# Reflections of a QR in three pieces a step instead of five or four, and a wider spacing of those pieces

## The chip, the core and the metric

The kernel runs on one core of a Trainium2 chip. The metric is device time in microseconds (us), the median of three runs; lower is better. Everything is float32. The core's engines, as the profile names them: PE (TensorE, matrix products), DVE (VectorE), ACT (ScalarE), POOL (GpSimd), and SP, whose queue issues most transfers. Each takes its instructions in the order in which the program leaves them; they wait for one another through semaphores.

## The reference, cut to what matters

Four blocks work one after the other on x (4 batches x 512 tokens x 288 features), with one condition vector for each batch: a transformer block with a mixture of four experts (two chosen for each token), a transformer block with a dense MLP, a rotation within a subspace, and another transformer block. The change touches only the third:

```python
def _L2_cond_ref(x, cond, P, W, b):
    U, _ = jnp.linalg.qr(P)                  # P is 288 x 64
    R = _rotation(cond, W, b)                # expm of a skew 64 x 64 matrix
    z = jnp.einsum('btn,nd->btd', x, U)
    z_rot = jnp.einsum('btd,bde->bte', z, R)
    return x + jnp.einsum('btd,nd->btn', z_rot - z, U)
```

U and R do not depend on x. So the kernel computes them beside the first two blocks. U comes from Householder reflections, 64 of them. For each, one needs the norm of what is left of a column (a sum of squares, then a square root, taken as a power of 0.5), a few scalars, and then the reflection of all later columns.

## The kernel before, in words

**Main work.** The attention of each block runs in 16 groups (4 batches x 4 groups of heads). A group has 8 slots (`k`), and each slot has four score products: two whose row maxima VectorE takes (line 875), two whose exponentials ScalarE takes (line 887). The scores rotate through four PSUM banks (tag `sc`); everything else on TensorE rotates through three (`de`). The products stand in an order fixed by hand: `mm` chains each matmul to the one before it. The first block's experts (`Experts`) work off 19 items of 256 gathered rows each. For an item the first layer is 9 products of 256 columns, each over two full blocks of features and a rest, and the second is 2 x 9 products of 288 columns. Their weights, `e0w`, and rows, `e0xs`, are fetched by indirect transfers that GpSimd issues (line 1818). The results are stored by SP (line 1904).

**Beside-work.** Two lists of generators, `beside` and `aside`, hold work that is done in between. `tick` (line 772) advances the first generator of `beside` to its next `yield`, and with `both` that of `aside` too. An attention ticks four times in each group, in slots 1, 3, 5 and 7, and four times in its first and last; that is 68 ticks. `Feed.went` counts the columns that the MLP or the experts stream, those counted being the products over full blocks of features, and ticks each time that `pace` columns have gone by. In the experts `pace` is 985 and `both` is true; in the dense MLPs it is 1000 and false. Item 0 of the experts is worked off without ticks. A piece of work emitted in a tick goes into each engine's queue at that place among the main work. `beside_of` and `in_turn` tie the first vector instruction of a piece, or the power on GpSimd, to what was last put on that engine by the main work; the other instructions are placed by a scheduler, which keeps dependencies and roughly the order of the program.

`beside` holds `rotation()`: the reflections (`reflections`, 64 columns), then U itself from the kept vectors (`subspace`, 64 steps), then a small product for each batch. The second half of the first block's modulation is put in front of it in group 4 of the first attention and takes five ticks; the last block's modulation stands behind it. `aside` holds the matrix exponential (`exponential`) and the second block's modulation. Beside-work that is left when the second block ends is drained there.

**One reflection**, `k`, in `reflections`: lines 604 to 607 form the sum of squares `rest` (by `dots`, line 555), `n2` and the sign; line 609 takes the power on GpSimd (`nrm`); lines 614 to 619 compute scalars on VectorE and leave two of them beside the row in `pT`; `reflector` (line 545) has SP spread that row over the partitions into `v`; two ticks later `reflect` reads `v` (line 549 first, then 555, 572 and 573). `inside[0]` is true while an attention runs. So a reflection takes five ticks inside an attention and four outside.

Of the kernel before, what the change touches and what calls it, by code (L numbers as in the profile page):

```python
# [45 lines left out]
def kernel(ctx: ExitStack, tc: tile.TileContext, a: dict, out: bass.AP):  # L46
# [21 lines left out]
    def bank(tag, name):  # L68
        return psum.tile([P, 512], F32, tag=tag, name=name, bufs=banks[tag])
# [30 lines left out]
    def beside_of(engine, instruction):  # L100
        if engine in taken:
            ordered(instruction.ins, taken[engine])

    def in_turn(engine, instruction):

        beside_of(engine, instruction)
        take(engine, instruction)
# [433 lines left out]
    def reflector(n, k):  # L541

        v = bgp.tile([RK, C + 2], F32, tag="v", name=f"{n}_{k}", bufs=4)
        r = RK - 1 - k
        nc.sync.dma_start(v[0:r, 0 : C + 2 - k], spread(pT[r : r + 1, k : C + 2], r))
        return v
# [5 lines left out]
    def dots(k, m, v, n):  # L552
        junk = bgp.tile([RK, C], F32, tag="junk", name=f"junk_{k}", bufs=1)
        w = small.tile([RK, 1], F32, tag="w", name=f"w_{k}")
        ins = nc.vector.tensor_tensor_reduce(
            out=junk[0:n, 0 : m.shape[1]],
            in0=m,
            in1=v,
            scale=1.0,
            scalar=0.0,  # L560
            op0=ALU.mult,
            op1=ALU.add,
            accum_out=w[0:n],
        )
        return w[0:n], ins

    def reflect(k, m, v, n):

        c = headed(k, v, n)
        w, _ = dots(k, m[0:n, k:C], v[0:n, 0 : C - k], n)  # L570
        w2 = small.tile([RK, 1], F32, tag="w2", name=f"w2_{k}")
        nc.vector.scalar_tensor_tensor(w2[0:n], w, -1.0, c, ALU.mult, ALU.mult)
        nc.vector.scalar_tensor_tensor(
            m[0:n, k:C], v[0:n, 0 : C - k], w2[0:n], m[0:n, k:C], ALU.mult, ALU.add
        )
# [3 lines left out]
    def reflections():  # L579

        nc.gpsimd.memset(back, 0.0)
        nc.gpsimd.affine_select(
            out=back,
            in_=back,
            compare_op=ALU.not_equal,
            fill=1.0,
            base=1 - RK,
            pattern=[[1, RK]],
            channel_multiplier=1,
        )  # L590
        ps = bank("de", "psback")
        nc.tensor.matmul(ps[0:RK, 0:C], lhsT=back, rhs=pT[:, 0:C], start=True, stop=True)
        nc.vector.tensor_copy(pT[:, 0:C], ps[0:RK, 0:C])
        for k in range(RK):
            n = RK - k

            def one(name):
                return small.tile([RK, 1], F32, tag=name, name=f"{name}_{k}")[0:n]


            alpha, tail = pT[0:n, k : k + 1], pT[0:n, k + 1 : C]
            hd, c = pT[0:n, C : C + 1], pT[0:n, C + 1 : C + 2]
            n2, nrm, sgn = one("n2"), one("nrm"), one("sgn")
            rest, ins = dots(k, tail, tail, n)
            beside_of("DVE", ins)
            nc.vector.scalar_tensor_tensor(n2, alpha, alpha, rest, ALU.mult, ALU.add)  # L606
            nc.vector.tensor_scalar(sgn, alpha, 0.0, 2.0, ALU.is_ge, ALU.mult)
            yield
            in_turn("POOL", nc.gpsimd.tensor_tensor(nrm, n2, phalf[0:n], ALU.pow))  # L609
            yield  # L610


            sn, den, rden = one("sn"), one("den"), one("rden")
            beside_of("DVE", nc.vector.scalar_tensor_tensor(sn, sgn, -1.0, nrm, ALU.add, ALU.mult))
            nc.vector.tensor_add(hd, alpha, sn)
            nc.vector.tensor_mul(den, sn, hd)
            nc.vector.tensor_scalar_max(den, den, TINY)
            nc.vector.reciprocal(rden, den)
            nc.vector.scalar_tensor_tensor(c, rest, 0.0, rden, ALU.is_gt, ALU.mult)
            if n > 1:  # L620
                v = reflector("v", k)
                yield
                yield
                reflect(k, pT, v, n - 1)
                if inside[0]:
                    yield

    def subspace():

# [118 lines left out]
    def rotation():  # L748
        yield from reflections()
        yield from subspace()  # L750
        for b in range(B):
            ps = bank("de", f"psue_{b}")
            for kc in range(KC):
                nc.tensor.matmul(
                    ps[0:CP, kc * RK : (kc + 1) * RK],
                    lhsT=uT[halves[b // HB], kc * CP : (kc + 1) * CP],
                    rhs=ef[halves[b // HB], b % HB, :],
                    start=True,
                    stop=True,
                )  # L760
            nc.vector.tensor_copy(
                ue[:, b, :, :],
                ps[0:CP, 0 : KC * RK].rearrange("p (k j) -> p k j", j=RK),
            )
            yield
# [4 lines left out]
    inside = [False]  # L770
# [436 lines left out]
    class Feed:  # L1207
# [7 lines left out]
        pace, both = 1200, False  # L1215
# [141 lines left out]
    class Dense(Feed):  # L1357


        pace = 1000  # L1360
# [47 lines left out]
    class Experts(Feed):  # L1408
# [5 lines left out]

        pace, both = 985, True
        width = SW
        loads_from, loads_every, loads_at = 2, 1, (0, 2, 4, 6)
        last_pieces = ("XXX", "XX", "", "AAA", "")  # L1420
# [846 lines left out]
```

## Time and profile before

| what | us |
|---|---|
| median of three runs | 2022.97 (2016.03 to 2024.35) |
| the profiled execution | 2016.98 |
| its span, first to last instruction | 2015.0 |
| TensorE busy / mean granted clock | 1913.5 / 0.975 |
| VectorE busy | 1076.7 |
| ScalarE busy | 746.6 |
| GpSimd busy | 539.9 |
| first attention | about 30 to 419 |
| experts | 419 to 925 |
| second attention | 925 to 1310 |
| its dense MLP | to 1460 |
| rotation of x | to 1495 |
| third attention | 1495 to 1850 |
| its dense MLP | to 2015 |

The stages overlap a little at their ends. In the profile a line starts with the engine or with the tile that is written and read: `v<-pT` is the transfer that spreads a row. "A <- B: t, n, m" in a list of waits means that A waited for B for t us in all, n times, at most m us. A line of busy time by stretch gives for each engine the busy us and, in brackets, the instructions, in the order PE, PEld (loading of weights), DVE, ACT, POOL; then the clock granted to TensorE as a share of the full one, the share of DMA engines that were busy, and GB/s. A float32 matmul stands in the profile as two records. A line of a timeline starts with the start and the duration; in square brackets stand the idle time of the engine just ahead of it and what ended it.

### The profile page before, as it was taken

How to read it: one execution, taken by the hardware profiler on the slowest of the kernel's cores; microseconds unless marked ns; L12 is line 12 of the kernel's file. 1: busy time of each engine (PE TensorE's matmuls, PEld its weight loads, DVE VectorE, ACT ScalarE, POOL GpSimd, SP SyncE). 2: the span in 40 equal slices, each digit the busy share in tenths (PEclk: the TensorE clock that was granted, in tenths of full speed). 3: DMA queues.
4: the chain of work that ended last, by engine and by line, in shares of the span. 5: the costliest groups of instructions: out<-in, count | busy, mean ns of one | idle time of the engine just before them, and what ended most of it. 6: DMA issues, size and time to landing. Idle time of an engine off the chain costs nothing. (4 is left out here: it accounts for less than half of the span.)

```text
span 2015.0 us, 28809 instructions
## 1 busy us (share of the span) xinstructions
PE 1913.5 (95%) x10602; PEld 1008.9 (50%) x10602; DVE 1076.7 (53%) x3129; ACT 746.6 (37%) x1367; POOL 539.9 (27%) x776
## 2 busy tenths in 40 slices
PE   7999999998889899899999999999999999999998
PEld 4434443365556667675334443456554344433555
DVE  5666777623434333446777777454155666554211
ACT  1554555332211222232555544511124555555220
POOL 4111121443233445652332122211400211213101
PEclk9999999898889999899999999999999999999999
DMA  7521121346444665651111111220000111111000
GB/s 155 118 54 21 22 45 46 106 117 195 138 138 148 197 203 179 187 183 37 42 44 38 36 37 40 56 61 21 21 1 10 28 29 36 28 26 23 19 15 24
DMA packets 95166, 147.27 MB, mean 73 GB/s; under 512 B 33267, under 2 KB 72798, under 8 KB 95026
## 3 DMA queue, kind: packets, MB, share of 16 engines
q1 hardware_dynamic: 68690, 66.16, 14.3%
q0 software_dynamic: 26224, 79.27, 13.2%
q8 instruction: 84, 1.38, 0.3%
q14 instruction: 56, 0.46, 0.1%
q10 hardware_dynamic: 112, 0.01, 0.0%
HBM read 114.66 MB, written 20.54 MB: 67 GB/s over the span
## 5 line engine op out<-in xcount | busy, mean ns | idle before, releaser
L875 DVE TENSOR_REDUCE max<-a3m 128x1 f32<-128x512 f32 x256 | 164.6, 685 | 128.1 <-PE a3s L78 120.8
L78 PE MATMUL e0h<-e0hT,e0w 128*128 128x256 f32 (+1 forms) x1026 | 213.6, 416 | 13.1 <-DMA e0w<-w1c,wrow 10.2
L875 DVE TENSOR_REDUCE max<-a0m 128x1 f32<-128x512 f32 x256 | 165.3, 683 | 90.2 <-PE a0s L78 78.1
L875 DVE TENSOR_REDUCE max<-a1m 128x1 f32<-128x512 f32 x256 | 165.7, 684 | 75.3 <-PE a1s L78 68.0
L887 ACT ACTIVATE a0p<-a0s 128x512 f32<-128x512 f32 x256 | 140.2, 596 | 144.5 <-PE a0s L78 144.1
L887 ACT ACTIVATE a1p<-a1s 128x512 f32<-128x512 f32 x256 | 140.9, 596 | 139.4 <-PE a1s L78 139.2
L887 ACT ACTIVATE a3p<-a3s 128x512 f32<-128x512 f32 x256 | 140.0, 596 | 137.6 <-PE a3s L78 137.6
L78 PEld LDWEIGHTS e0h<-e0hT,e0w 128*128 128x128 f32 (+1 forms) x1026 | 149.6, 196 | 70.0 <-issue 47.2
L78 PE MATMUL e0o<-e0w,e0hm 128*128 128x288 f32 x648 | 178.6, 427 | 0.1
L78 PE MATMUL a0m<-a0qk,a0qk 32*128 32x512 f32 x512 | 159.1, 645 | 7.9 <-DVE max L875 6.8
L78 PE MATMUL a1m<-a1qk,a1qk 32*128 32x512 f32 x512 | 157.5, 640 | 7.8 <-DVE max L875 6.5
L78 PE MATMUL a0s<-a0qk,a0qk 32*128 32x512 f32 x512 | 161.0, 653 | 0.0
L78 PE MATMUL a1s<-a1qk,a1qk 32*128 32x512 f32 x512 | 158.4, 640 | 0.2 <-DVE u L549 0.2
L78 PE MATMUL a3m<-a3qk,a3qk 32*128 32x512 f32 x512 | 151.2, 643 | 6.8 <-DVE max L875 5.5
L78 PE MATMUL a3s<-a3qk,a3qk 32*128 32x512 f32 x512 | 153.0, 644 | 0.3 <-DVE a3qk L929 0.3
L78 PEld LDWEIGHTS e0o<-e0w,e0hm 128*128 128x128 f32 x648 | 125.5, 198 | 37.3 <-issue 2.7
L1281 ACT ACTIVATE e0hm<-e0h,e0w 128x256 f32<-128x256 f32 x162 | 75.6, 473 | 181.6 <-PE e0h L78 138.8
L609 POOL TENSOR_TENSOR nrm<-n,phalf 64x1 f32<-64x1 f32 (+31 forms) x64 | 36.4, 569 | 321.6 <-DVE n L606 296.4
L78 PEld LDWEIGHTS a1m<-a1qk,a1qk 32*128 32x128 f32 x512 | 46.9, 183 | 73.2 <-DVE max L875 41.1
L78 PEld LDWEIGHTS a0m<-a0qk,a0qk 32*128 32x128 f32 x512 | 47.3, 184 | 69.2 <-DVE max L875 41.2
L549 DVE COPY v<-v 63x1 f32<-63x1 f32 (+62 forms) x63 | 8.8, 139 | 134.5 <-DMA v<-pT 122.0
L78 PE MATMUL f1h<-f1hT,w 128*128 128x512 f32 (+1 forms) x216 | 79.9, 614 | 0.4 <-ACT f1hT L504 0.4
(496 smaller groups left out, 3241.1 us busy)
## 6 DMA issues: line engine op xcount, KB each, us to landing
eo<-e0r SPq DMA_DIRECT2D x50, 144.0 KB
ada<-in_ada SPq DMA_DIRECT2D x18, 324.0 KB
wr<-in_wrot SPq DMA_DIRECT2D x16, 288.0 KB
g<-gates SPq DMA_DIRECT2D x24, 144.0 KB
xm<-e0m SPq DMA_DIRECT2D x6, 576.0 KB
w1c<-in_w SPq DMA_DIRECT2D x20, 144.0 KB
w<-in_w SPq DMA_DIRECT2D x6, 432.0 KB
x<-in_x SPq DMA_DIRECT2D x16, 144.0 KB
```

Of the source, the lines that this page charges most:

```text
L78: ins = nc.tensor.matmul(*args, **kwargs).ins
L549: beside_of("DVE", nc.vector.tensor_copy(v[0:n, 0:1], v[0:n, C - k : C - k + 1]))
L609: in_turn("POOL", nc.gpsimd.tensor_tensor(nrm, n2, phalf[0:n], ALU.pow))
L875: take("DVE", nc.vector.tensor_reduce(m[:, t, i, D : D + 1], ps, AX.X, ALU.max))
L887: take("ACT", nc.scalar.activation(p, ps, AF.Exp, scale=D**-0.5))
L1281: nc.scalar.activation(self.hms[i][f], ps[r][:, 0 : self.width], func, bias=b1(f)),
```

## The change

Three edits, all in the order of the work; what is computed stays the same.

1. The `yield` between the sums and the power is gone: the power is emitted in the same tick as the sums.
2. The `yield` behind a reflection inside an attention is gone: the sums of the next column come in the same tick as the reflection, inside an attention as outside.
3. `pace` of the experts is 1500 columns instead of 985, for both lists.

So a reflection now has three ticks everywhere: reflection of the column before with the sums and the power; the scalars and the transfer of `v`; an empty one.

```diff
             nc.vector.scalar_tensor_tensor(n2, alpha, alpha, rest, ALU.mult, ALU.add)
             nc.vector.tensor_scalar(sgn, alpha, 0.0, 2.0, ALU.is_ge, ALU.mult)
-            yield
             in_turn("POOL", nc.gpsimd.tensor_tensor(nrm, n2, phalf[0:n], ALU.pow))
             yield
...
                 yield
                 yield
                 reflect(k, pT, v, n - 1)
-                if inside[0]:
-                    yield
...
-        pace, both = 985, True
+        pace, both = 1500, True
         width = SW
```

## The prediction

> **What bounds the kernel now.** I read the page's busy shares first, then busy time by stage, then who TensorE waited for in the stage that stands out, then what held the engine it waited for.
>
> ```profile
> PE 1913.5 (95%) x10602; PEld 1008.9 (50%) x10602; DVE 1076.7 (53%) x3129; ACT 746.6 (37%) x1367; POOL 539.9 (27%) x776
> PEclk9999999898889999899999999999999999999999
> ...
> 419.00:925.00 506.00, 457.35 (x2670) 328.85 (x2672) 202.55 (x933) 120.65 (x276) 214.14 (x246) 0.93 0.56 167
> 1495.00:1850.00 355.00, 345.91 (x2106) 146.25 (x2106) 217.38 (x413) 178.39 (x315) 63.70 (x105) 0.99 0.12 25
> ```
>
> TensorE sets the end: 95% busy, 101.5 us idle. Of that idle time 48.7 us lie in 419 to 925 us, the experts, and the clock column dips there too (mean 0.93). In windows of 2 us, one minus the clock, times the time TensorE worked, comes to 29.5 us there. So some 78 of the experts' 506 us are stall or half clock. The third attention, which carries no reflection, loses 9 us in 355.
>
> ```profile
> PE e0h L78 <- DMA e0w<-w1c,wrow: 10.2, 3, 4.5
> PE psmod L410 <- DVE rows L397: 7.2, 2, 4.5
> PE e0xt L78 <- DVE rv L684: 5.9, 1, 5.9
> PE e0xt L78 <- DVE skew L717: 4.3, 1, 4.3
> PE e0xt L78 <- DVE ef L743: 2.9, 1, 2.9
> ...
> PE psr L675 <- DMA wr<-in_wrot: 2.5, 1, 2.5
> ```
>
> These are TensorE's waits inside the experts. Vector work of the exponential and of the modulation was late. Why it was late stands in VectorE's and GpSimd's waits of the same stretch:
>
> ```profile
> DVE v L549 <- DMA v<-pT: 120.8, 30, 10.0
> ...
> POOL nrm L609 <- DVE n L606: 160.2, 35, 15.5
> ```
>
> and in VectorE's timeline around one stall (TensorE idle 4.25 us until 558.91):
>
> ```profile
> 552.88 0.15 DVE L619 SCALAR_TENSOR_TENSOR pT<-w,rden 44x1 f32<-44x1 f32 x1
> 558.49 0.15 DVE L549 COPY v<-v 43x1 f32<-43x1 f32 x1 [5.46 <-DMA v<-pT]
> 558.57 0.60 DVE L717 TENSOR_TENSOR skew<-up,psup 64x128 f32<-64x128 f32 x2
> ```
>
> VectorE finished the reflection's scalars, the row went out to be spread, the next vector instruction in line needed it, and `skew`, which TensorE wanted, stood behind. The reflections are light; their place in line is what costs.
>
> **Pace.** The experts stream 18 items x (9 x 2 x 256 + 2 x 9 x 288) = 176,256 columns: at 985 a tick 178 ticks, at 1500 117. Over 490 us that is 2.74 us a tick before and, at the same length, 4.2 us after. Where nothing but the stream runs, one item (9 x 6 e0h records, 36 e0o) takes 54 x 0.208 + 36 x 0.276 = 21.1 us (213.6/1026 and 178.6/648 of the page) for 9,792 columns, so 2.1 and 3.2 us a tick. Two ticks lie between the issue of `v` and its use, before and after: 4.2 us become 6.4 in pure stretches, 5.5 become 8.4 on average. From the end of L619 to `v` being there took 3.0 us (738.20 to 741.24) to 6.5 (505.18 to 511.71), and the scalars ahead of it 1.06 (730.09 to 731.15). So the old gap was too short and the new one fits most transfers. A whole reflection is a chain of 1.98 (reflection and sums, 727.36 to 729.34) + 0.75 (norm) + 1.06 + 3.0 to 6.5 = 6.8 to 10.3 us, against ticks of 4 x 2.1 = 8.4 before and 3 x 3.2 = 9.6 after.
>
> **Stalls behind `v`.** I take 2.5 us, between the 2.2 and 2.9 gained, off each of VectorE's waits. Of the listed 133 us (30 waits for the DMA, 3 put to issue) about 55 remain. Of TensorE's stalls behind them (5.86, 4.25, 2.87, 4.49, 1.80, 0.79, 2.67, 1.44, together 24.2) 3.36, 1.75, 0.37, 1.99 and 0.17 remain: **16.5 us saved**. Bounds 0 and 24.2.
>
> **The `wr` wait.** Its last load also has two ticks; 2.45 us against 2.9 gained on average: **2.5 saved**, and its dip of 3.2.
>
> **Clock.** Dips that follow these vector stalls cost 1.8, 3.8, 1.7, 1.7, 1.7, 1.7 = 12.4 us. Three of the stalls vanish (5.1 saved), three shrink (half of 7.3): **8.7 saved**, 11.9 with `wr`. [...]
>
> **Gathers.** The power is moved one tick ahead on GpSimd, past the gathers of one tick (0.95 us each plus 0.30), and now waits there for 1.98 us of vector work of its own tick. Behind it stand gathers of w1, w2 and tokens; TensorE waits for w1 (10.2 us, dips of 2.8, 1.7 and 3.0). Against that GpSimd waits less for late sums: the gather in front of the stall at 843.53 was issued after a wait of 6.73 us for them. Bounds -6 (each of the three stalls longer by those 1.98) and +17.7; nearest is the row with 6.73, of which `v`'s lateness was 2.27: a third, **+5.3**.
>
> **First attention.** It has 63 ticks for this work (68 less 5 of the modulation). Five a reflection gave 12, three give 21. One costs 0.14+0.41+0.07+0.15+0.47 to reflect, 0.41+0.07+0.21+0.14 to sum, 0.89 of scalars: 2.96 us, so 8 to 9 more make 24 to 27 us of VectorE. From 50 to 350 us it is busy 214.5 of 300, so 85 us of cover are there, and TensorE lost about 5 in all. Reflect and sums now come as one lump of 2.07 where they were 1.24 and 0.83. If the cover is missing, a lump costs what follows. Bounds 0 and 15; **-3**, as the rows of that stage show few waits. `v` is issued on SP 8 to 9 more times (0.76 us each), ahead of the denominators' loads, which have several slots in hand; in the experts `v` keeps its place on SP ahead of the next eo stores, and there are 39 of it instead of 45.
>
> **Second attention and after.** Ticks 181 to 248: four reflections, then 56 steps of U (1.24 us each) where there were 35 and six or so reflections. 21 x 1.24 - 3 x 2.96 = 17 us more on VectorE over 385, where 1000 to 1200 us shows 150.5 busy of 200 and TensorE 196.4: nothing. The dense block has 8 U steps left instead of 29; its one wait (2.4) moves or stays: nothing. All beside-work ends well ahead of the rotation.
>
> [...] The row: the sum at 842.41 took 1.45 us, not 0.41, with a GpSimd add running. [...] I take nothing.
>
> **Sum.** 16.5 + 2.5 + 11.9 + 5.3 - 3 = 33 us. 2016.98 - 33 = 1984 for the profiled execution. The median shown, 2022.97, stands 6.0 above it; half of that goes on top: **1987 us**.
>
> **Rivals.**
> (a) The waits only move: vector work with its pieces closer together re-forms behind `v`, or gathers behind the early power. For it: landing times up to 10 us, and -6 above. Against it: 3 x 3.2 us exceed the chain's usual 7 to 9. Time: 16.5 + 11.9 mostly gone, 2012 to 2025, say 2018.
> (b) Slower: lumps in the first attention stall the row maxima. Place: slots that also carry norm or projection work. A row maximum can be late by some 1.3 us before TensorE feels it (four score banks, 0.65 us a matmul, two in hand). Price: between 363 and 367 us a lump of routing stalled TensorE 1.60 + 0.56 and the dip behind cost 3.2, so 5.4 us each. It decides from six lumps on (33/5.4); ten give 2017 - 33 + 54 = 2038. Against it: at 217.2 a reflection of 1.34 us with two pieces of norm of 0.66 around it left no wait.
> (c) All of it goes, gathers too: 24.2 + 2.5 + 15.6 + 17.7 = 60: 1957 to 1963.
>
> **How the numbers follow.** Main case 0.62 (1968 to 2008 its own range), (a) 0.13, (b) 0.16, (c) 0.09. About 0.5% (10 us) is what a measurement of this kernel tells from no change; the three runs shown lie 8 us apart. Faster: main, (c), and a little of (a), 0.74. Same: the rest of (a) and the edge of (b), 0.10. Slower 0.16. The range leaves out half of (c) below and most of (b) above: 1960 to 2026.
>
> **What would show it.** Right: `v`'s waits in the experts at some 55 us instead of 121, TensorE idle there under 30 instead of 49 with mean clock at 0.95 or more, no wait on rv or skew over 3.5 us, 21 powers before 405 us, the U steps starting near 1000 instead of 1106. Wrong: TensorE waits on the row maxima in the first attention above 15 us (b); e0w waits above 16 us (the power in GpSimd's line); or unchanged `v` waits (a).

## The result, and the profile after

The changed kernel takes 2003.86 us in the median of 14 runs (1994.50 to 2016.25), beside 2023.12 for the kernel before (14 runs). The ratio is 0.9912 with a 95% interval of 0.9890 to 0.9933: faster by 19 us, where 33 (36 against the median) were forecast. On another chip, later, the same kernel stood at 0.9973 (0.9960 to 0.9986) of the kernel before, 7 us faster. The profiled execution took 1994.5 us, the lowest of the 14; a second profile, from the later occasion, took 2024.2, the highest of 22. Both are used below: they bracket the kernel, while the profile of the kernel before lies 6 us below its median.

The page's first rows after the change:

```profile
PE 1904.4 (96%) x10602; PEld 1004.3 (50%) x10602; DVE 1080.2 (54%) x3129; ACT 748.7 (38%) x1367; POOL 541.9 (27%) x776
PEclk9999999988899999999999999999999999999999
```

Who TensorE waited for in and just after the experts (425 to 925 us), the list that was led by gathers, `rows`, `rv`, `skew` and `ef`:

```profile
PE e0xt L78 <- DMA e0xs<-xm,token: 6.1, 1, 6.1
PE e0o L78 <- ACT e0hT L1878: 4.5, 2, 2.3
PE e0p1k L78 <- DVE e0p1h L1739: 3.7, 2, 2.4
PE e0xt L78 <- DVE m L725: 3.6, 1, 3.6
PE psmod L410 <- DVE rows L397: 2.1, 1, 2.1
PE e0h L78 <- DMA e0w<-w1c,wrow: 1.8, 2, 1.1
```

VectorE's and GpSimd's longest waits on the reflections in the experts:

```profile
DVE v L549 <- DMA v<-pT: 72.2, 21, 7.6
```

```profile
POOL nrm L608 <- DVE n L606: 131.4, 30, 15.5
```

The stalls on `rv` and `ef` are gone, that on `skew` fell from 4.3 to 0.6 us, those for gathered weights fell from 10.2 to 1.8, and VectorE waits 72 us for `v` instead of 121 (133 with what is put to issue). New are a wait of 6.1 us for gathered rows, one on `m`, also of the exponential, of 3.6, and 4.5 us behind ScalarE. So the experts did in the main what was said. The first attention did not. Busy time by stage, first attention and experts:

```profile
30.00:421.00 391.00, 374.97 (x2246) 160.79 (x2246) 290.15 (x814) 179.82 (x321) 88.69 (x138) 0.97 0.27 64
421.00:902.00 481.00, 452.23 (x2743) 329.28 (x2740) 188.76 (x850) 128.13 (x288) 215.94 (x246) 0.95 0.59 177
```

Before, the first attention was

```profile
30.00:406.00 376.00, 366.37 (x2250) 158.29 (x2250) 267.45 (x694) 178.86 (x321) 84.10 (x130) 0.98 0.28 65
```

It carries the same matrix products, but is 15 us longer: 6 us more idle and 9 us more "busy". The stages, each counted from its first product of the main work to that of the next (score, expert, dense or rotation product), are (us, one profile each):

| kernel | first attention | experts | second attention | its dense MLP | rotation | third attention | rest |
|---|---|---|---|---|---|---|---|
| before | 375.7 | 519.2 | 361.4 | 173.9 | 35.8 | 352.6 | 166.5 |
| changed | 390.6 | 481.0 | 368.0 | 171.0 | 35.8 | 349.4 | 166.5 |
| changed, second profile | 390.7 | 495.9 | 374.0 | 171.2 | 39.1 | 354.2 | 166.6 |

The experts gained 38 us (23 in the second profile); the first attention gave 15 back in both, the second attention 7 (13).

The two profiles of the changed kernel differ by 30 us. Half clock, summed as in the prediction (in windows of 2 us, one minus the clock, times the time TensorE worked), took 30 us of the first and 51 of the second, and 45 before; 10 us more are stalls in the experts.

### The profile page after: what moved, and what is told of

Read it like the earlier page. It is cut to its first block, busy times and chain, and to the rows that moved or that the text cites. A ratio compares the mean times of both kernels' runs of the same rounds, so it can differ in the third digit from the quotient of the medians.

```text
span 1992.7 us, 28800 instructions
## 1 busy us (share of the span) xinstructions
PE 1904.4 (96%) x10602; PEld 1004.3 (50%) x10602; DVE 1080.2 (54%) x3129; ACT 748.7 (38%) x1367; POOL 541.9 (27%) x776
## 4 chain that ended last, share of the span: by engine, by line
PE 69%; DVE 7%; DMA 3%; POOL 1%; ACT 1%; issue 1%; SPq 0%; POOLq 0%; DVEq 0%; ACTq 0%
PE e0h L78 8%; PE e0o L78 7%; PE a3m L78 7%; PE a1m L78 7%; PE av L78 6%; PE a3psqk L78 4%; PE f3h L78 4%; DVE max L872 4%; PE a1psqk L78 4%; PE f1h L78 4%; PE f3o L78 4%; PE f1o L78 3%; DMA e0w<-w1c,wrow 1%; PE a1pp L78 1%; PE a3psv L78 1%; PE a3pp L78 1%
## 5 line engine op out<-in xcount | busy, mean ns | idle before, releaser
L78 PE MATMUL e0h<-e0hT,e0w 128*128 128x256 f32 (+1 forms) x1026 | 200.7, 408 | 3.0 <-DMA e0w<-w1c,wrow 1.8
L78 PE MATMUL a0m<-a0qk,a0qk 32*128 32x512 f32 x512 | 167.5, 648 | 13.1 <-DVE max L872 10.7
L78 PE MATMUL a1m<-a1qk,a1qk 32*128 32x512 f32 x512 | 163.0, 641 | 9.1 <-DVE max L872 8.0
L78 PEld LDWEIGHTS e0h<-e0hT,e0w 128*128 128x128 f32 (+1 forms) x1026 | 143.3, 191 | 54.2 <-issue 32.3
L78 PE MATMUL a0s<-a0qk,a0qk 32*128 32x512 f32 x512 | 169.2, 656 | 0.0
L78 PE MATMUL f3h<-f3hT,w 128*128 128x512 f32 (+1 forms) x216 | 79.4, 613 | 0.4 <-ACT f3hT L504 0.4
```

The costliest lines, as they stand in the source:

```text
L78: ins = nc.tensor.matmul(*args, **kwargs).ins
```

## The experiments

Each kernel here computes all of the reference. Lines with a plus are added to the changed kernel, or to the kernel before where the text says so. Stage times are read as in the table above, from one profile each; the ratios are to the kernel before.

**Fewer ticks in the first attention, and none where the routing runs.**

```diff
-    attention(0, w, mod, 1e-6, feed, 4, then=work)
+    attention(0, w, mod, 1e-6, feed, 2, then=work)
```

> The changed kernel with two ticks a group instead of four in the first attention: 29 ticks of its own there instead of 63, so 9 to 10 reflections instead of 21. If the number of reflections sets what the first attention loses (15 us for 9 more, 1.7 each), it is 18 to 20 us shorter than in the changed kernel (first e0h at about 402 instead of 421), the experts stay near 481 us, and the run is at 1986 to 1990 against a median of 2004. If the loss comes from meetings with the routing in groups 11 to 15 alone, a part of the meetings stays and the gain is 4 to 8 us. If my working of the prediction was right and reflections cost the first attention 3 us in all, nothing moves by more than 5 us.

Measured: 0.9926 (0.9892 to 0.9960), 2006.6 us, 10 reflections in the first attention, which took 383.5 us: 7 less, not 18 to 20. But this profile lost 17 us to half clock there, that of the changed kernel 10, so without the clock the gain is 14, and the run doesn't settle whether the number of reflections is the price. In all it is slower than the 1986 to 1990 expected.

```diff
-                    if k % 2 and (k + 3) % (gaps // ticks) == 0:
+                    if k % 2 and (k + 3) % (gaps // ticks) == 0 and not (l == 0 and r >= 11):
                         tick()
```

> The changed kernel without ticks in groups 11 to 15 of the first attention, where the routing of the experts runs on VectorE: 14 reflections there instead of 21. If meetings with the routing are the price, the last five groups go from 127.5 us to about 115 and the ten before stay at 224, in all 12 us or more off (1990 to 1993 against 2004). If it is the number alone, 7 x 1.7 = 12 us too, but the half-tick kernel then gains half as much again; the two together tell.

Measured: 0.9880 (0.9847 to 0.9914), 2000.5 us. From one `a0qk` subtraction to the next, the last five groups took 117.4 us (127.4 changed, 118.4 before): 10 of the 12 us expected. The ten groups ahead took 232.5 instead of 224.3, with two stretches of half clock (48 to 60 and 138 to 150 us, 9.7 us) that the changed kernel's profile doesn't have; so the run as a whole missed the 1990 to 1993 expected. Nine of the 15 us that the first attention lost lie where the routing runs.

**The lump.** Reflection and sums in two slots again, inside attentions only; power and pace as changed:

```diff
                 reflect(k, pT, v, n - 1)
+                if inside[0]:
+                    yield
```

> The changed kernel with the yield behind a reflection inside an attention put back: reflection (1.24 us) and sums (0.83) in two slots instead of one lump of 2.07, and so four ticks a reflection there, 15 in the first attention instead of 21. If lumps are the price, the first attention comes back to the length before (first e0h at 406). If only the number counts, it gives 6 x 1.7 = 10 us, e0h at 411. Experts at 481 either way; median 1992 to 1996.

Measured: 0.9855 (0.9819 to 0.9890), 1994.05 us. The first attention takes 376.8 us, with 16 powers issued in it. That is the length before. Its experts took 502.0 us, not the 481 expected. Once more, beside the changed kernel on one chip:

> The changed kernel once more, for a second profile and beside the version with the sums apart. Its first profile stands at 1994.5, the lowest of 14 runs with a median of 2004, so I expect a longer one: experts at 485 to 500 instead of 481, first attention at 390 again, since all five kernels with the lump and full ticks or half of them show 383 to 400 there. Median 2000 to 2007.

> The version with the sums apart once more, on the same chip as the changed kernel: if the lump costs what the stages show (14 us in the first attention, some 5 in the second, whatever the experts do), it is 8 to 20 us faster than the changed kernel. If the gain of its first four runs was chance, the two are within 5 us.

Measured: the changed kernel 2015.13 us, 0.9973 (0.9960 to 0.9986), 8 us above what I expected; sums apart 1983.86 us, 0.9812 (0.9783 to 0.9840). The difference is 31 us, more than I expected, and more than the 14 us of the first attention. The profiles put 5 more in the experts, 8 in the second attention and 8 in the three stages after it (dense MLP, rotation, third attention), where the two programs have no reflection left; 7 of those last 8 are half clock. The version with the sums apart beats both kernels there, and the kernel before in both series. Its first attention and experts:

```profile
30.00:406.00 376.00, 366.94 (x2244) 158.90 (x2242) 274.11 (x739) 178.76 (x320) 85.37 (x133) 0.97 0.28 65
406.00:897.00 491.00, 454.53 (x2736) 330.39 (x2732) 189.77 (x850) 127.85 (x290) 216.63 (x248) 0.95 0.58 174
```

Then the lump alone, put into the kernel before (power a tick later, pace 985):

```diff
                 reflect(k, pT, v, n - 1)
-                if inside[0]:
-                    yield
```

> The kernel before with the second edit alone: sums in the tick of the reflection inside the attentions, power a tick later, pace 985. The experts never had this yield, so they stay at 510 to 525. If the lump is the price, the first attention goes from 375.7 to 385 to 395 and the run to 2033 to 2040. If the price needs the early power or more reflections than 16 there, it stays at 377 and the run at 2023.

Measured: 1.0068 (1.0050 to 1.0087), 2034.8 us; first attention 390.6, experts 518.1. One edit gives as long a first attention as the whole change does and touches nothing in the experts. Of the 14.9 us, 6.7 are more half clock than before; in the changed kernel that share is 1.8. Over all profiles, the seven without the lump have first attentions of 375.7 to 376.9 us, the five with it and with all ticks 390.6 to 400.0. Its VectorE timeline shows where it hurts. The rows that the experts' routing needs are scaled (lines 1508 and 1512), and the lump comes behind them:

```profile
331.24 0.94 DVE L1508 SCALAR_TENSOR_TENSOR e0m<-x,e0m1mv,e0m1sc 128x288 f32<-128x288 f32 x2
332.09 0.94 DVE L1512 SCALAR_TENSOR_TENSOR e0m<-e0m,e0m1rstd,e0m1sh 128x288 f32<-128x288 f32 x2
332.95 0.14 DVE L549 COPY v<-v 52x1 f32<-52x1 f32 x1
...
333.69 0.68 DVE L873 TENSOR_REDUCE max<-a0m 128x1 f32<-128x512 f32 x1
334.29 0.49 DVE L573 SCALAR_TENSOR_TENSOR pT<-v,w,pT 52x277 f32<-52x277 f32 x1
334.81 0.44 DVE L555 CUSTOM_DVE_ANT_0 junk<-pT 52x275 f32<-52x275 f32 x1
...
335.43 0.68 DVE L873 TENSOR_REDUCE max<-a0m 128x1 f32<-128x512 f32 x1
```

TensorE, same kernel:

```profile
334.42 0.69 PE L78 MATMUL a0m<-a0qk,a0qk 32*128 32x512 f32 x1 [1.28 <-DVE max L873]
336.16 1.22 PE L78 MATMUL a0m<-a0qk,a0qk 32*128 32x512 f32 x1 [0.25 <-DVE max L873]
```

Two row maxima start 1.7 us apart among the pieces of the lump instead of back to back, the first of them late behind the scaling and the lump's first pieces. TensorE waits 1.28 and 0.25 us for score banks, and half clock follows (1.22 us for a product of 0.69; 3.2 us lost between 334 and 342).

**Which edit mends the experts.** The old pace, with both yields gone:

```diff
-        pace, both = 1500, True
+        pace, both = 985, True
```

> The changed kernel with the old pace of 985 columns in the experts: only the two yields are gone. If the gap of two ticks behind the transfer of v is what mended the experts, VectorE's waits for v there are back at 110 us or more for the reflections that are left, TensorE idles 45 us or more, and the experts take 510 to 520 us: slower than the kernel before by what the first attention lost, 2035. If taking the power out of a tick of its own did it, the experts stay at 481 to 490.

Measured: 1.0232 (1.0195 to 1.0269), 2072.6 us; experts 550.2 us. Slower than expected: 31 us more than before the change, with VectorE's waits for `v` at 107 us. The first attention took 400.0 us with the order of work of the changed kernel there (390.6); 5 of those 9 us are half clock. The power alone, in the kernel before:

```diff
-            yield
             in_turn("POOL", nc.gpsimd.tensor_tensor(nrm, n2, phalf[0:n], ALU.pow))
```

> The kernel before with only the power moved into the tick of its sums, pace 985 and both other yields as they were: three ticks a reflection in the experts, two of them still between the transfer of v and its use. If the pace is what helps, this is no faster than before: v's waits stay above 100 us and the experts take 530 to 550 (work comes faster than its chain of 7 to 10 us runs, 3 x 2.1), 2045 to 2070 in all. If the power's earlier place helps, the experts come below 510 and the run below 2015. First attention about 377 in both.

Measured: 1.0239 (1.0199 to 1.0279), 2077.2 us; experts 561.2, first attention 376.9; both the experts and the run are slower than expected. Who TensorE waited for in its experts:

```profile
PE e0h L78 <- DMA e0w<-w1c,wrow: 23.5, 6, 9.9
PE psmod L410 <- DVE rows L397: 10.5, 3, 7.6
```

Faster emission without the wider spacing makes both kinds of stall worse, gathers (10.2 before) and vector work. Both of these kernels also put more pieces into the experts: 43 and 48 reflections and already 49 and 34 steps of U, where the kernel before has 45 and none. The pace alone, in the kernel before; the dense MLP ticks more often here, so that the longer list of pieces ends in time:

```diff
-        pace, both = 985, True
+        pace, both = 1500, True
...
-        pace = 1000
+        pace = 480
```

> The kernel before with only the pace at 1500, all yields kept; the dense block ticks each 480 columns so that the work still ends there. If the wider gap alone mends the experts, they take 480 to 502 us as in the changed kernel, with v's waits at 80 or below, and the first attention stays at 375 to 377; in all 1990 to 2000 unless the dense block with twice the ticks loses more than 5 us. If the power must move too, the experts stay at 510 or more.

Measured: 1.0036 (1.0006 to 1.0066), 2036.6 us. First attention 376.0, experts 488.5 (31 less than before), dense MLP 213.4 instead of 173.9. So the pace alone gives a gain of the experts as large as the whole change does, and the total loses it again: with four- and five-tick reflections at that pace all 64 steps of U are left to the dense MLP, which is 39 us longer (the leftover work and the twice as many ticks are not separated). Nor are the two lists: the pace spaces out the exponential and the modulation as well as the reflections, and no run widened one list alone. It also leaves 29 reflections in the experts, not 45; but the changed kernel gains with 39 in a shorter stage, so fewer pieces are not all of it. VectorE's waits for `v` in its experts:

```profile
DVE v L549 <- DMA v<-pT: 35.1, 11, 4.7
```

The changed kernel with the power a tick later again (dense pace 600):

```diff
+            yield
             in_turn("POOL", nc.gpsimd.tensor_tensor(nrm, n2, phalf[0:n], ALU.pow))
...
-        pace = 1000
+        pace = 600
```

> The changed kernel with the power again one tick behind its sums, so four ticks a reflection everywhere: 15 lumps of reflection and sums in the first attention, 29 reflections in the experts at 1500 columns. The dense block ticks each 600 columns so that the longer work still ends there. If the lump of reflection and sums is what the first attention pays for, it stays long (385 or more from the first a0m to the first e0h, against 375.7 before and 390.6 changed), unlike the 376.8 with the sums apart. If what it pays for is the power that stands early in GpSimd's line, it comes back to 376 or 377. Experts: 481 to 502 if the pace is what mends them, 515 if the power's place is.

Measured: 1.0006 (0.9988 to 1.0024), 2024.3 us; first attention 390.9, experts 485.6, dense MLP 196.9. The lump keeps its price without the early power. For the experts the power's place shows no worth at this pace; what it buys is 39 reflections there in place of 29, and with that the dense MLP.

**Other spacings**, both with the sums apart; 2000 columns with a dense pace of 600, and 1250:

```diff
-        pace, both = 1500, True
+        pace, both = 2000, True
...
-        pace = 1000
+        pace = 600
```

> Sums apart in the attentions, the power with its sums, and a pace of 2000 in the experts, 600 in the dense block: a gap of 8.6 us in pure stretches, beyond nearly all transfers of v. If the gap is still what limits the experts, v's waits fall below 40 us, the experts take 470 to 480, and the run is at 1980. If the remaining stalls there are others (gathers, ScalarE, the exponential), the experts stay at 485 to 502 and the run at 1990 to 1996.

Measured: 1.0016 (1.0000 to 1.0032), 2027.0 us; `v` waits down to

```profile
DVE v L549 <- DMA v<-pT: 23.7, 7, 6.8
```

but the experts at 504.7 us, above both ranges expected, and the dense MLP at 196.1. Beyond 1500 the waits for `v` go on falling and nothing is gained: the largest of TensorE's waits there is 8.7 us in all, which the profile puts to issue, and what is behind it stays open.

```diff
-        pace, both = 1500, True
+        pace, both = 1250, True
```

> Sums apart, power with its sums, pace 1250: three ticks are 3 x 2.7 = 8.1 us in pure stretches, between the 6.4 of pace 985 (experts 561) and the 9.6 of pace 1500 (502 in its first profile). If the chain of 7 to 10 us is what must fit, the experts lie between, at 505 to 530, and the run at 2000 to 2025. If 8.1 us is enough, they stay at 481 to 502 and the run at 1990 to 1997.

Measured: 1.0004 (0.9985 to 1.0023), 2020.2 us; experts 515.6. Between 561.2 (985) and 491.1 or 502.0 (1500), as expected of a chain that must fit its spacing.

## Why the prediction was right or wrong

Two terms of the sum failed: the first attention, put at -3 us, lost 15, and the second attention, put at nothing, lost 7 (13 in the second profile). They took back more than half of what the experts gave (all of it in the second profile). By stages the first profile gains 22 us: 38 in the experts, -15 and -7 in the attentions, and 6 in the stages after them, where nothing was forecast and 5 us are half clock. The step that failed in both terms is the same: idle time of VectorE, summed over a stage, was taken as cover for added pieces, whatever their size and place.

**The experts: right.** The step gave 36 us (16.5 + 2.5 + 11.9 + 5.3); the two profiles of the changed kernel show 38 and 23, the pace alone 31, the power apart 34. That the first of these lies within 2 us of the forecast is luck, as the second shows. The cause, a spacing too narrow for the chain, was named rightly: experiments with the old spacing lose, those with the new one gain; how much of it is the reflections' spacing and how much the exponential's is not shown. By terms: waits for `v` were to fall to 55 us and fell to 72 and 77; TensorE's idle time was to fall below 30 and is 28.8 and 39.0. The gathers of weights gave more than their term, 10.2 to 1.8 and 1.4 us, but gathered rows took 6.1 and 4.9 of it back, so that 2 to 4 us of stall were gained where 5.3 were forecast with the dips (a third of 17.7 is 5.9, not 5.3). The moved power was to cost or gain by its place in GpSimd's line; at the new pace neither shows.

**The clock: near the forecast.** Half clock in the experts fell from 29.6 us to 18.6 and 21.9. That is 11.0 and 7.7 saved, where 11.9 was forecast (without the gathers' dips). Taking short stalls into the sum was right in kind: in the kernel before, the stall of 2.45 us that ends at 474.53 has clock 0.50 behind it (476 to 480 us); in the changed kernel 1.07 and 0.93 us of stall, ending at 305 and 307, are followed by half clock from 308, and the second profile, with the same order of work, loses the same 1.7 us there. But the length of a stall doesn't settle it. The kernel with a pace of 2000 has clock 0.81, 0.50 and 0.83 in the three windows from 44 to 50 us, behind 0.40 us of idle time between 42 and 46; the changed kernel has waits of 0.40 and 0.46 us there (ending at 44.16 and 48.99) and keeps clock 1.00.

**The first attention: the term that failed.** "-3, as the rows of that stage show few waits" measured -15, in two profiles of the changed kernel and in the lump alone: the upper bound of the term. Two things were wrong in it. First, the cover: 85 us of free VectorE are an average, but the row maxima come every slot and the lump goes into one. Its pieces hold them apart. Second, the reading of the rows. The 5 us that TensorE lost were those of 50 to 350 us; over the whole stage it was 10 idle and 8 of half clock. And the listed waits of row-maximum products say little here. Before and after the change they are

```profile
PE a0m L78 <- DVE max L875: 6.8, 10, 1.6
```

```profile
PE a0m L78 <- DVE max L872: 10.7, 14, 2.0
```

while the stage grew by 15. The rest sits in "busy" (366.4 to 375.0, of which 1.8 are clock): score products that start together in other slots come one after the other behind a wait for a row maximum. In the changed kernel's first attention:

```profile
305.01 0.69 PE L78 MATMUL a0m<-a0qk,a0qk 32*128 32x512 f32 x1 [1.07 <-DVE max L872]
305.54 0.59 PE L78 MATMUL a0m<-a0qk,a0qk 32*128 32x512 f32 x1
...
313.81 0.69 PE L78 MATMUL a0m<-a0qk,a0qk 32*128 32x512 f32 x1
313.83 0.69 PE L78 MATMUL a0m<-a0qk,a0qk 32*128 32x512 f32 x1
```

The first two start 0.53 us apart, the other two 0.02. Counted over the stage, score records start four at a time (each within 0.05 us of the one before) 184 times before the change and 183 with the sums apart, but 175 times in the changed kernel and 174 with the lump alone. So the sign I had set for rival (b), waits above 15 us, did not show it.

Rival (b) named the mechanism and the place, slots that carry other vector work; its price, 5.4 us a lump from six lumps on, holds only for the worst. Over 21 lumps it is 0.7 us each. By groups: 9.1 us in the last five, 4.8 in the ten before, 1.0 around them.

**VectorE beside GpSimd: I took nothing, and there is something.** The changed kernel in group 12, VectorE:

```profile
301.30 1.35 DVE L2069 TENSOR_TENSOR e0r0tie<-e0r0lg 128x64 f32<-128x64 f32 x1
302.58 0.16 DVE L2075 TENSOR_REDUCE e0r0top<-e0r0lg 128x4 f32<-128x16 f32 x1
302.69 0.83 DVE L2070 TENSOR_TENSOR e0r0tie<-e0r0tie,earlier 128x64 f32<-128x64 f32 x1
303.44 0.78 DVE L2077 TENSOR_TENSOR e0r0pe<-e0r0lg,e0r0top 128x16 f32<-128x16 f32 x1
...
304.88 0.20 DVE L2072 TENSOR_REDUCE rank<-e0r0ahead 128x16 f32<-128x64 f32 x1
```

GpSimd:

```profile
301.18 0.62 POOL L608 TENSOR_TENSOR nrm<-n,phalf 50x1 f32<-50x1 f32 x1 [3.53 <-DVE e0r0lg L1576]
301.79 0.78 POOL L990 TENSOR_TENSOR a0bg<-g,bp 128x288 f32<-128x288 f32 x1
302.64 3.11 POOL L994 TENSOR_TENSOR x<-x,a0bg 128x288 f32<-128x288 f32 x4
```

With the sums apart, `e0r0tie` and its product with `earlier` took

```profile
295.35 0.22 DVE L2071 TENSOR_TENSOR e0r0tie<-e0r0lg 128x64 f32<-128x64 f32 x1
...
295.60 0.23 DVE L2072 TENSOR_TENSOR e0r0tie<-e0r0tie,earlier 128x64 f32<-128x64 f32 x1
```

GpSimd stood 3.53 us before the power, the five additions queued behind it could not start until then, and ran when the routing ran. The three instructions with two inputs in SBUF took 1.35, 0.83 and 0.78 us (0.22, 0.23 and 0.17 with the sums apart, where nothing ran on GpSimd from 292.64 to 298.81 us); the reduction at 304.88, which has one input and ran beside one of the additions, took 0.20 (0.21 with the sums apart). That the second input decides is not shown: `e0r0ahead` at 304.14, with two, took 0.21 while the additions ran (0.22 with the sums apart). The group took 27.4 us, 22.2 before. I had looked at what follows the power on VectorE, in an attention the row maximum (0.68 us at 304.28, while the additions ran, as elsewhere), and not at what is queued behind it on GpSimd. The lump alone, without this meeting, loses the same 15 us with this group at 22.4, so the meeting isn't the cause of the whole.

**The second attention: nothing forecast, 7 and 13 lost.** The prediction had the pieces right (4 reflections, 56 steps of U where there were 35) and took their cost for nothing because VectorE and TensorE had room on average. The profiles say otherwise (us; half clock summed as above):

| kernel | reflections there | steps of U | length | half clock |
|---|---|---|---|---|
| before | 6, apart | 35 | 361.4 | 1.7 |
| changed | 4, lumps | 56 | 368.0 | 1.6 |
| changed, second profile | 4, lumps | 56 | 374.0 | 10.1 |
| sums apart | 9, apart | 32 | 360.7 | 1.7 |
| sums apart, pace 1250 | 1, apart | 64 | 367.9 | 1.7 |
| sums apart, pace 2000 | 17, apart | 0 | 357.9 | 4.7 |
| power apart | 17, lumps | 0 | 358.2 | 1.7 |

With 64 steps of U and no lump the stage is as long as in the changed kernel; with 32 it is 7 us shorter. That is 0.2 us a step, so 21 more steps are worth an estimated 5 of the 7 us. In the second profile half clock makes 8 more. What the lumps cost here stays open: 17 of them took 358.2 us, the same number apart 357.9, but the kernels of the first two experiments, with 15 and 10 lumps and fewer steps of U than the changed one, stood at 366 without half clock.

**The offset.** Half of the 6 us between profile and median was added; the first profile of the changed kernel lies 9 below its median, so the distance of one profile from its median was worth less than that.

## What to carry to other kernels

Idle time of an engine is cover only in pieces of the right size: ask for each moved piece how long it holds back the short, periodic instruction that the bound engine needs, and not how much is free in sum (here 85 us, and the stage grew by 15). Where matmuls overlap, compare the length of a stage, since late inputs show as busy time as much as waits (here 9 us busy and 6 idle). A chain with a transfer in it should be emitted no faster than it can run (here 7 to 10 us against 6.4, 8.1 and 9.6), and when it is spaced out, the number of pieces must shrink with it, or the work lands where nothing hides it (the dense MLP here, 39 us).

## What the runs showed of the hardware

- Half clock follows short stalls, but not each time: behind two of 1.07 and 0.93 us within 3 us it came in both profiles of the changed kernel (308 to 312 us); behind 0.40 us at 44 us it came in the kernel with a pace of 2000 (clock 0.50 from 46 to 48 us) and not in the changed one (1.00 from 40 to 62, with another 0.46 us ending at 49).
- With the same order of work, the first attention took 390.6, 390.7 and 400.0 us in three profiles (two of the changed kernel, one with the old pace), and the experts, with their gathers, 481.0 and 495.9 in two. Of the 30 us between the two profiles of the changed kernel 20 are half clock.
- Three small two-input VectorE instructions that ran beside GpSimd instructions took 4 to 6 times as long as with the sums apart, where GpSimd stood idle (1.35 us against 0.22, 0.83 against 0.23, 0.78 against 0.17); a fourth, at 304.14, took 0.21 against 0.22, and a reduction with one input 0.20 against 0.21.
